# Two non-local attention blocks on one core: other slots for the weight-preparation steps, and the odd pair normalised one slot later

## The chip, the cores and the metric

The kernel runs on one core of a Trainium2 chip. The metric is the device time of one launch in microseconds (us), the median of several runs.

## The reference

Four images of 128 channels by 96 x 96 pixels pass through two layers, one after the other. Each layer is a non-local block:

```
g_x   = maxpool2(conv1x1(x, g_w, g_b))          # 64 channels, 2304 keys
theta = conv1x1(x, theta_w, theta_b)            # 64 channels, 9216 queries
phi   = maxpool2(conv1x1(x, phi_w, phi_b))      # 64 channels, 2304 keys
attn  = softmax(theta^T phi)                    # per query, over the 2304 keys
y     = attn g_x
out   = batchnorm(conv1x1(y, W_w, W_b)) + x     # inference batch norm: a scale and a shift
```

Everything is float32. Batch norm folds into the weights: W is scaled by `inv = gamma * rsqrt(var + eps)`, and all the biases become one shift per channel.

## The kernel before, in words

There are eight blocks, an image with a layer each, in the order of `ORDER`: image 0 layer 0, image 1 layer 0, image 0 layer 1, and so on. A block's 9216 queries are split into nine **pairs** of 1024 queries, 72 pairs in all. For a pair, the 2304 keys are 18 tiles of 128. A **slot** handles two key tiles of one pair, so a pair takes nine slots (NB), and a **cycle** is 18 slots: an even pair in slots 0 to 8 and an odd pair in slots 9 to 17. There are 36 cycles, 648 slots. The main loop runs over the slots `t`, with `s` the slot in its cycle and `q` the first pair of the cycle; what it writes down is the order of each engine's instructions, which no scheduler changes (the schedule is manual).

In each slot TensorE (PE) makes the scores of two key tiles (`sc`, L600), ScalarE (ACT) takes their exponential into one of six `exp` buffers (L605), VectorE (DVE) adds them to the running denominators (`sum`, L612 and L614), and PE multiplies the values of the slot before into `av` (L622). Around this, other work is hung on fixed slots:

- **Units.** While a block runs, the keys and values of the next one are made in six units (`Unit`), two a cycle in the cycles that have any. A unit has four PE stages (L450, L456) in slots 15, 16, 0, 2 (even units) or 7, 8, 10, 12 (odd units), each followed by DVE additions that read its two PSUM banks: L472; L483 twice; L493, L494, L495; L505, L506. Then come two poolings (L510) and DVE transposes (L552). The sums of pixels that the stages read are made by DMAs of SP (L430 to L435) and by accumulating DMAs of GpSimd (POOL, L427).
- **The end of a pair.** ACT copies `av` to `halves` (L629). DVE turns and adds the denominators (`turn`, L672, L673, slots 8 and 9 for the even pair, 4 and 5 for the odd one of the cycle before), adds the two halves of `av` (L705, slots 12 and 2), inverts (L685 to L690, slots 13 and 6), and SP spreads the inverses over the partitions (L694, L698). Then `normalise` multiplies them in (L708, slot `NORM`: 1 for the even pair of the cycle before, 10 for the odd one), PE projects with W (`multiply`, L714, slots 3 and 13), ACT adds the shift (L725) and a POOL DMA adds the result to x (L729).
- **The two PSUM banks** of the tag `misc` serve the unit stages, the theta projections (L277) and the W projections in turn: L714 of slot 3 follows the fourth unit stage of slot 2 in them, and L714 of slot 13 that of slot 12, so it can't start before L505 and L506 have read them.
- **Weights.** The layers' weights are loaded and then turned and scaled in short **steps**, which a dictionary `after` hangs on the end of slots. Layer 0: `mixed` in slots 7, 8, 9 and W in slots 10 to 14 of cycle 0 (`make_scale` L187 to L189, two steps of four 32x32 transposes L150, an ACT copy L228, `make_shift` L235 to L243). Layer 1: 14 steps (`gphi` 4, `mixed` 3, `theta` 2, W 5), three a cycle in slots 2, 7 and 11 of cycles 1 to 5. A step of `gphi`, of `theta` and two of those of W are four DVE transposes; `mixed` is three ACT copies, five small DVE operations and one ACT copy. `load_W` of layer 1 (SP, L171 and L173) stands at slot 16 of cycle 0; it overwrites a buffer that `make_shift` of layer 0 reads.

Within a slot, DVE gets its work in this order: the additions, with those of a unit stage after the first of them; `normalise`, `turn`, `add_halves`, `invert`; the poolings and transposes of units; the steps.

```
for i, step in enumerate(ws[0].steps_W()):
    after[10 + i] = [step]
...
for i, step in enumerate(steps):
    after[CYCLE + i // 3 * CYCLE + (2, 7, 11)[i % 3]] = [step]
```

Of the kernel before, what the change touches and what calls it, by code (L numbers as in the profile page):

```python
# [48 lines left out]


TURNS, HALVES, INVERT = (8, 4), (12, 2), (13, 6)
NORM, PROJECT = (1, 10), (3, 13)
SQ = 32
EXPS = 6
WARM = (5, 3)
CYCLE = 2 * NB
# [6 lines left out]
def shifted_blocks(ctx: ExitStack, tc: tile.TileContext, x: bass.AP, layers, out: bass.AP, flag):  # L63
# [24 lines left out]
    nc = tc.nc  # L88
# [706 lines left out]
    ws = [Layer(l, p) for l, p in enumerate(layers)]  # L795
# [65 lines left out]
    after = {8: [other_cols]}  # L861
    for i, step in enumerate(ws[0].steps_mixed()):
        after[7 + i] = after.get(7 + i, []) + [step]
    for i, step in enumerate(ws[0].steps_W()):
        after[10 + i] = [step]
    after[9] += [lambda: ws[1].load_gphi((nc.sync, nc.sync)), lambda: ws[1].load_theta(nc.sync)]
    after[16] = [lambda: ws[1].load_W(nc.sync)]
    steps = [lambda i=i: late_steps("gphi", i) for i in range(4)]
    steps += [lambda i=i: late_steps("mixed", i) for i in range(3)]
    steps += [lambda i=i: late_steps("theta", i) for i in range(2)]  # L870
# [3 lines left out]
    def late_steps(what, i):  # L874
        if i == 0:
            made[what] = getattr(ws[1], f"steps_{what}")()
        made[what][i]()

    for i, step in enumerate(steps):
        after[CYCLE + i // 3 * CYCLE + (2, 7, 11)[i % 3]] = [step]  # L880

    keys = {2 * j: (0, FIRST + j) for j in range(NB - FIRST)}
    squares = {k: [(1, k)] for k in range(4)} | {5: [(2, k) for k in range(4)]}
# [37 lines left out]
    for t in range(total + 1):  # L921
# [6 lines left out]
        if t in keys:  # L928
            n, i = keys[t]
# [16 lines left out]
        if t < total:  # L946
# [3 lines left out]
            if t in loads:  # L950
                b, i = loads[t]
# [333 lines left out]
def nonlocal_blocks(tc: tile.TileContext, x: bass.AP, layers, out: bass.AP):  # L1285
    with tc.tile_pool(name="flag", bufs=1) as pool:
        flag = pool.tile([1, 1], I32, name="flag")
        shifted_blocks(tc, x, layers, out, flag)
        bad = tc.nc.values_load(flag[0:1, 0:1])
        with tc.If(bad > 0):  # L1290
            general_blocks(tc, x, layers, out)
# [30 lines left out]
```

## Time and profile before

| | |
|---|---|
| time, median of 3 runs | 2484.16 us (2483.57 to 2484.65) |
| the profiled execution's own time | 2483.91 us |
| its span in the profile | 2482.1 us |
| granted TensorE clock in it | 0.999 |
| PE, busy | 2472.2 us, 23391 matmuls |
| PE weight loads, busy | 1602.5 us |
| DVE, busy | 2192.5 us, 2947 instructions |
| ACT, busy | 1667.2 us, 1836 instructions |
| POOL, busy | 254.2 us, 286 instructions |

The profile is of one execution. Matmuls overlap each other and the profile models their ends, so the busy time of PE says that it nearly always had something in it and not that it worked at its full pace; for that, the starts of its matmuls are counted in a stretch. "PEld" is the load of a matmul's weights. "L614 <- ACT exp L605" in a view of waits means that the instruction of line 614 was released by one of ACT of line 605. A time in a view is counted from the start of the span.

### The profile page before, as it was taken

The page shows a single profiled execution, that of the slowest core. Times are in us where ns is not written, and L with a number is a line of the kernel's source. Part 1 is how long each engine was busy: PE and PEld are TensorE (multiplying, and loading weights), DVE is VectorE, ACT ScalarE, POOL GpSimd, SP SyncE. Part 2 cuts the span into 40 slices and gives each one's busy share as a digit, 9 for nine tenths or more (in the row PEclk, how much of TensorE's full clock was granted, in tenths as well). Part 3 has the DMA queues.
Part 4 walks back from the last instruction along what each step waited for, and adds up shares of the span by engine and source line. Part 5 has one row for each costly group of instructions (what it writes and reads, how often), then busy time and mean ns, then how long its engine had stood idle before and what let it go on. Part 6 is the DMA issues. An engine that isn't in the chain of part 4 may idle for free.

```text
span 2482.1 us, 56196 instructions
## 1 busy us (share of the span) xinstructions
PE 2472.2 (100%) x23391; PEld 1602.5 (65%) x23391; DVE 2192.5 (88%) x2947; ACT 1667.2 (67%) x1836; POOL 254.2 (10%) x286
## 2 busy tenths in 40 slices
PE   9999999999999999999999999999999999999998
PEld 5556555666666666666666666666666666666665
DVE  7999989998789988999878998899988899877778
ACT  6666666666667666666666666666666666666665
POOL 0011011100011101111001110111101111000000
PEclk9999999999999999999999999999999999999999
DMA  6366456543356636664346663665424565333334
GB/s 186 45 83 101 52 84 79 81 47 27 36 74 99 101 38 93 89 89 78 44 47 79 84 99 44 94 83 68 49 26 51 77 85 88 42 44 44 44 37 60
DMA packets 101038, 171.72 MB, mean 69 GB/s; under 512 B 16030, under 2 KB 78120, under 8 KB 100776
## 3 DMA queue, kind: packets, MB, share of 16 engines
q1 hardware_dynamic: 65664, 94.11, 31.0%
q0 software_dynamic: 34944, 73.88, 19.6%
q8 instruction: 185, 3.03, 0.5%
q14 instruction: 77, 0.63, 0.1%
q10 hardware_dynamic: 168, 0.07, 0.0%
HBM read 19.21 MB, written 18.87 MB: 15 GB/s over the span
## 4 chain that ended last, share of the span: by engine, by line
PE 94%; DVE 4%; DMA 1%; issue 1%; ACT 0%; SPq 0%; DVEq 0%; POOL 0%; POOLq 0%; ACTq 0%
PE av L622 42%; PE sc L600 42%; PE unit_ps L450 3%; PE theta_ps L277 2%; PE W_ps L714 2%; DVE sum L614 2%; DMA halves<-stage 1%; PE unit_ps L456 0%; PE gphi_ps L329 0%; ACT exp L605 0%; PE gphi_ps L277 0%; DVE four L685 0%; DVE turned L672 0%; DVE stage L510 0%; DVE parts L673 0%
## 5 line engine op out<-in xcount | busy, mean ns | idle before, releaser
L605 ACT ACTIVATE exp<-sc,nshift 128x1024 f32<-128x1024 f32 x1296 | 1391.6, 1112 | 732.8 <-PE sc L600 702.6
L614 DVE TENSOR_TENSOR sum<-sum,exp 128x1024 f32<-128x1024 f32 x1151 | 1408.1, 1223 | 205.5 <-ACT exp L605 149.3
L600 PE MATMUL sc<-theta,phi 64*64 64x512 f32 x10368 | 1459.7, 589 | 0.9 <-ACT exp L605 0.9
L622 PE MATMUL av<-exp,gT 64*64 64x512 f32 x10368 | 1386.2, 589 | 0.0
L622 PEld LDWEIGHTS av<-exp,gT 64*64 64x64 f32 x10368 | 717.5, 133 | 379.4 <-issue 49.8
L600 PEld LDWEIGHTS sc<-theta,phi 64*64 64x64 f32 x10368 | 716.2, 133 | 371.2 <-issue 41.8
L427 POOL DMA_DIRECT2D sums<-x x84 | 81.2, 1140 | 1029.6 <-DMA sums<-x 496.9
L729 POOL DMA_DIRECT2D x<-halves x70 | 62.7, 895 | 1056.3 <-ACT halves L725 1034.5
L612 DVE TENSOR_TENSOR sum<-exp,exp 128x1024 f32<-128x1024 f32 x72 | 88.0, 1222 | 30.0 <-ACT exp L605 29.8
L673 DVE TENSOR_REDUCE parts<-turned 128x16 f32<-128x512 f32 x142 | 97.4, 686 | 4.9
L672 DVE STREAM_TRANSPOSE turned<-sum 128x512 f32<-128x512 f32 x142 | 100.2, 706 | 0.5
L629 ACT COPY halves<-av 128x1024 f32<-128x1024 f32 x71 | 72.0, 1014 | 35.4 <-PE av L622 35.4
L427 POOL DMA_DIRECT2D sums<-sums x84 | 90.9, 1082 | 32.5 <-issue 10.3
L714 PE MATMUL W_ps<-halves,WT 64*64 64x512 f32 x568 | 90.8, 590 | 0.4 <-DVE stage L505 0.4
L277 PE MATMUL theta_ps<-x,thetaT 64*64 64x512 f32 x560 | 89.9, 589 | 0.0
L725 ACT ACTIVATE halves<-W_ps,shift 128x512 f32<-128x512 f32 x140 | 88.6, 692 | 0.9 <-PE W_ps L714 0.9
L450 PE MATMUL unit_ps<-sums,mixed 64*64 64x384 f32 x504 | 78.9, 482 | 0.0
L510 DVE TENSOR_REDUCE stage<-stage 128x192 f32<-128x768 f32 x84 | 77.9, 941 | 0.0
L552 DVE STREAM_TRANSPOSE gT<-stage 32x192 f32<-32x192 f32 (+1 forms) x224 | 71.5, 319 | 3.8
L685 DVE STREAM_TRANSPOSE four<-parts 32x32 f32<-32x32 f32 x284 | 56.4, 198 | 2.9
L708 DVE TENSOR_TENSOR halves<-halves 128x512 f32<-128x512 f32 x71 | 48.8, 687 | 8.9 <-DMA halves<-stage 8.8
L714 PEld LDWEIGHTS W_ps<-halves,WT 64*64 64x64 f32 x568 | 39.7, 133 | 23.0 <-DVE stage L505 2.2
(113 smaller groups left out, 812.7 us busy)
## 6 DMA issues: line engine op xcount, KB each, us to landing
x<-halves POOLq DMA_DIRECT2D x70, 512.0 KB, 4.7
halves<-stage SPq DMA_DIRECT2D x284, 64.0 KB
out_dram<-x SPq DMA_DIRECT2D x35, 512.0 KB
sums<-x SPq DMA_DIRECT2D x42, 384.0 KB
sums<-x SPq DMA_DIRECT2D x84, 192.0 KB
sums<-x POOLq DMA_DIRECT2D x84, 192.0 KB, 4.3
sums<-sums POOLq DMA_DIRECT2D x84, 192.0 KB, 4.6
x<-in_x_dram SPq DMA_DIRECT2D x18, 768.0 KB
```

Source lines behind the costliest of these rows:

```text
L277: nc.tensor.matmul(out, lhsT=lhsT, rhs=rhs, start=step == 0, stop=step == 1)
L427: nc.gpsimd.dma_start(out=dst, in_=src, accum_op=ALU.add)
L450: nc.tensor.matmul(bank[ts(c, CI), :UN], lhsT=lhsT, rhs=rhs[:, c, :], start=True, stop=True)
L600: nc.tensor.matmul(ps[ts(c, CI), ts(h, QT)], lhsT=self.blk.keys_of(k, c, h), rhs=self.th[ts(h, CI), :], start=True, stop=True,)
L605: nc.scalar.activation(e, ps, AF.Exp, bias=nshift)
L612: nc.vector.tensor_add(self.sum, self.es[0], e)
L614: nc.vector.tensor_add(self.sum, self.sum, e)
L622: nc.tensor.matmul(self.av[ts(h, CI), ts(r, QT)], lhsT=self.blk.gT[ts(r, CI), k, :], rhs=e[ts(r, CI), ts(h, QT)], start=(k == 0), stop=(k ...
L672: nc.vector.transpose(self.turned, self.sum[:, ts(h, QT)])
L673: nc.vector.tensor_reduce(self.parts[:, ts(h, QT // SQ)], self.turned.rearrange("p (b k) -> p b k", k=SQ), AX.X, ALU.add,)
L714: nc.tensor.matmul(self.pss[h][ts(c, CI), :], lhsT=self.blk.w.W[ts(h, CI), ts(c, CI)], rhs=self.y[ts(h, CI), :], start=True, stop=True,)
L725: nc.scalar.activation(self.halves[:, ts(h, QT)], self.pss[h], AF.Identity, bias=self.blk.w.shift,)
```

## The change

Three things move; no instruction is added or removed.

- `make_shift` of layer 0 goes from slot 14 to slot 17 of cycle 0, and `load_W` of layer 1 goes with it from slot 16 to slot 17.
- The 14 steps of layer 1 stand two a cycle in slots 1 and 17, in cycles 1 to 7, where they stood three a cycle in slots 2, 7 and 11, in cycles 1 to 5.
- The odd pair of the cycle before is normalised in slot 11 and not in slot 10, in every cycle from 1 on.

```
-NORM, PROJECT = (1, 10), (3, 13)
+NORM, PROJECT = (1, 11), (3, 13)
...
     for i, step in enumerate(ws[0].steps_W()):
-        after[10 + i] = [step]
+        after[(10, 11, 12, 13, 17)[i]] = [step]
     after[9] += [lambda: ws[1].load_gphi((nc.sync, nc.sync)), lambda: ws[1].load_theta(nc.sync)]
-    after[16] = [lambda: ws[1].load_W(nc.sync)]
+    after[17] += [lambda: ws[1].load_W(nc.sync)]
...
     for i, step in enumerate(steps):
-        after[CYCLE + i // 3 * CYCLE + (2, 7, 11)[i % 3]] = [step]
+        after[CYCLE + i // 2 * CYCLE + (1, 17)[i % 2]] = [step]
```

## The prediction

> **What bounds the kernel now.** I read the page first, then the timeline of ACT at the cycles' first exponentials, then the waits of PE, then single slots.
>
> ```profile
> PE 2472.2 (100%) x23391; PEld 1602.5 (65%) x23391; DVE 2192.5 (88%) x2947; ACT 1667.2 (67%) x1836; POOL 254.2 (10%) x286
> ...
> PE 94%; DVE 4%; DMA 1%; issue 1%; ACT 0%; SPq 0%; DVEq 0%; POOL 0%; POOLq 0%; ACTq 0%
> ```
>
> PE is always busy and makes 94% of the chain that ended last. Whether a busy PE is at its pace shows in the cycles' lengths. The chain of work has 16 matmuls of 512 columns in 1.72 us, 0.1075 each, so a slot (32) takes 3.44 and a cycle's 18 slots 61.9; its theta and W projections are 32 more, 3.4: 65.4. The cycle without units from 575.06 to 640.29 took 65.23. The one from 706.49 has six unit stages of 8 matmuls of 384 columns and two of 8 of 192, worth (36 + 6) x 0.1075 = 4.5: 69.9 by count, 69.76 measured. So an ordinary cycle is PE's work at full pace, with no wait to win. Now the early cycles beside ordinary ones of the same work:
>
> ```profile
> 88.69 1.12 ACT L605 ACTIVATE exp<-sc,nshift 128x1024 f32<-128x1024 f32 x1 [1.31 <-PE sc L600]
> 160.41 1.11 ACT L605 ACTIVATE exp<-sc,nshift 128x1024 f32<-128x1024 f32 x1 [1.31 <-PE sc L600]
> 230.70 1.11 ACT L605 ACTIVATE exp<-sc,nshift 128x1024 f32<-128x1024 f32 x1 [1.31 <-PE sc L600]
> 300.32 1.11 ACT L605 ACTIVATE exp<-sc,nshift 128x1024 f32<-128x1024 f32 x1 [1.31 <-PE sc L600]
> 366.52 1.11 ACT L605 ACTIVATE exp<-sc,nshift 128x1024 f32<-128x1024 f32 x1 [1.31 <-PE sc L600]
> 436.52 1.11 ACT L605 ACTIVATE exp<-sc,nshift 128x1024 f32<-128x1024 f32 x1 [1.31 <-PE sc L600]
> ...
> 706.49 1.11 ACT L605 ACTIVATE exp<-sc,nshift 128x1024 f32<-128x1024 f32 x1 [1.31 <-PE sc L600]
> 776.25 1.11 ACT L605 ACTIVATE exp<-sc,nshift 128x1024 f32<-128x1024 f32 x1 [1.31 <-PE sc L600]
> 846.00 1.11 ACT L605 ACTIVATE exp<-sc,nshift 128x1024 f32<-128x1024 f32 x1 [1.31 <-PE sc L600]
> 914.78 1.11 ACT L605 ACTIVATE exp<-sc,nshift 128x1024 f32<-128x1024 f32 x1 [1.31 <-PE sc L600]
> ```
>
> The first lines open cycles 1 to 6, the last four cycles 10 to 13. Differences: cycle 1 took 71.72 against 69.76 for cycle 10, **1.96** too long; cycle 2 70.29 against 69.75 for cycle 11, **0.54**; cycle 3 69.62 against 68.78 for cycle 12, **0.84**; cycle 4 66.20, as cycle 9 (706.49 - 640.29), nothing; cycle 5 70.00 against 69.76, **0.24**. Together 3.58. In cycle 0, slot 16 took 4.39 (exponentials at 80.87 and 85.26), against 3.76 in cycle 9 (699.30 to 703.06): **0.63**. All of it lies where steps stand. What PE waits for in these places:
>
> ```profile
> PEld unit_ps L456 <- DVE stage L472: 3.6, 10, 0.9
> ...
> PEld W_ps L714 <- DVE stage L505: 2.2, 2, 1.1
> ```
>
> Both are PSUM banks that a late DVE frees late. In slot 12 and 13 of cycle 1:
>
> ```profile
> 138.10 0.85 DVE L150 STREAM_TRANSPOSE gphiT<-gphi_nat 32x32 f32<-32x32 f32 x4
> 138.98 1.23 DVE L614 TENSOR_TENSOR sum<-sum,exp 128x1024 f32<-128x1024 f32 x1
> 140.12 0.55 DVE L505 TENSOR_TENSOR stage<-stage,unit_ps 128x384 f32<-128x384 f32 x1
> ```
> ```profile
> 140.72 1.12 PE L714 MATMUL W_ps<-halves,WT 64*64 64x512 f32 x5 [0.23 <-DVE stage L505]
> ```
>
> The step of slot 11 (0.85) stands ahead of L505, and the projection starts 0.05 after L505 ends. In ordinary cycles L505 ends 1.1 to 1.6 before it.
>
> **The Trainium skill against this reading.** Trace Analysis, section Identifying the Most-Contended Engine, calls the busy time of matmuls a poor measure and wants the busy time of weight loads. By it PE (65%) would have a third of each cycle to win, some 24 us of 69.76, an estimate from that page. The count of matmuls above says that there is none; the sum goes by the count.
>
> **The change, part by part.**
>
> *make_shift from slot 14 to 17 of cycle 0.* Its five instructions hold DVE from 79.42 to 80.32, 0.90, just ahead of L472, which ends at 82.01 and is what L456 waits for at 82.06 (weight load 0.95 idle). Without them L472 ends at 81.1. PE's score matmul before that wait starts at 81.40, so L456 comes due 0.1 later and finds its bank free: the 0.63 goes.
>
> *Steps out of slots 2, 7 and 11.* DVE's delay builds up where its work has no gaps. A step in slot 2 still stood as 0.95 before slot 7's L472, a step of slot 7 came on top, and slot 11 lies right before L505. With the steps elsewhere DVE is where it is in cycles 10 to 12, and the 3.58 go.
>
> *Steps into slot 17.* In an ordinary cycle (slots 17, 0 and 1):
>
> ```profile
> 707.11 0.56 DVE L493 TENSOR_TENSOR stage<-stage,unit_ps 128x384 f32<-128x384 f32 x1 [0.34 <-PE unit_ps L450]
> ...
> 709.14 1.23 DVE L612 TENSOR_TENSOR sum<-exp,exp 128x1024 f32<-128x1024 f32 x1 [0.36 <-ACT exp L605]
> 711.77 2.56 DVE L614 TENSOR_TENSOR sum<-sum,exp 128x1024 f32<-128x1024 f32 x2 [1.40 <-ACT exp L605]
> ```
>
> The brackets are DVE idle. A pair's first key tile needs no addition, so there is room: 0.34 + 0.36 + 1.40 = 2.10 for a step of 0.85 to 1.2. L493 to L495 end some 0.5 later, at 709.2, and the stage that needs their banks is in slot 2, after 714. Cost 0, at most 0.5 each without that cover.
>
> *Steps into slot 1*, behind L708:
>
> ```profile
> 714.25 0.68 DVE L708 TENSOR_TENSOR halves<-halves 128x512 f32<-128x512 f32 x1
> 715.15 1.23 DVE L614 TENSOR_TENSOR sum<-sum,exp 128x1024 f32<-128x1024 f32 x1 [0.22 <-ACT exp L605]
> ...
> 719.23 2.56 DVE L614 TENSOR_TENSOR sum<-sum,exp 128x1024 f32<-128x1024 f32 x2 [0.19 <-ACT exp L605]
> ```
>
> Four transposes (0.85) here in cycles 1, 2, 5 and 6 put L505 and L506 back by 0.85 - 0.22 = 0.63. L714 of slot 3 starts at 718.47; L505 would end at 717.48, L506 at 717.94. Still 0.5 early: no wait. After the 0.19, 0.44 is left. In cycles 1 and 5 nothing takes it up before slot 7, since DVE runs without gaps from 721.70 on: L472 there ends at 738.29 and would at 738.73, L456 starts at 739.08 and its weight load, now at 739.08 too, would not wait. Cost 0 to 0.1 each; 0.44 each in two cycles if L456 needs more lead than 0.35. In cycles 3, 4 and 7 the step is ACT copies (0.24 to 0.30 each, three, one and one), under ACT's 1.3 of idle before an exponential.
>
> *Odd normalise from slot 10 to 11*, 0.69 in each cycle. Slot 10 also has L493 to L495; slot 11 then has it in place of a step. Between the two places stand two additions, so L505 in slot 12 has the same work before it. In a cycle like 12 DVE has no real gap from slot 9 to 14 and the swap is neutral; in one like 10 it may idle up to 0.6 in slot 11 that it used before, but L505 has at least 1.1 to spare. What waits for L708 is L714 in slot 13; L708 ended 4.0 to 6.2 before it, and the shift is a slot, 3.4: at least 0.6 is left. Gone are DVE's waits for the DMA that spreads the inverses (8.8 in 13 times), but no PE wait hung on them. Price 0; between a gain of 8.8 and a loss of 0.69 a cycle, I take 0 because ordinary cycles have nothing to win.
>
> *load_W at slot 17.* L173 must now wait for L237, which ends near 89.5, and took 2.32 on SP; behind it stands L430, issued at 89.34. It goes out 0.3 to 2.5 later, and with it POOL's sums (last of them at 104.43), which PE reads in slots 8 and 10, from 121 on. Cost 0. The weights themselves come two cycles later: `gphi` by slot 17 of cycle 2 for slot 15 of cycle 4, `mixed` by slot 1 of cycle 4 for slot 16, W by cycle 7 for cycle 9. All in time.
>
> **Sum.** 2483.91 (the profiled execution's own time) - 3.58 - 0.63 = 2479.7. The median shown lies 0.25 above that execution; I say **2479.8**.
>
> **Rivals.**
> - *Half of it stays.* The 0.44 that slot 1 leaves in DVE reaches L456 in slot 8 or, through the late L510 of slot 14, the unit stage of slot 15. For: that is how cycle 5 lost 0.24 from one step in slot 7. Against: the gaps above. Then some 2 of the 4.2 remain: 2481.8.
> - *More than the floor by count.* The records of matmuls are not complete, and 0.1 of PE idle a cycle in the 35 that move L708 could be hidden: 3.5 more, 2476.3. Against: cycle 8 agrees with its count.
> - *Slower.* L708 in slot 11 delays L505 by its full 0.69 where DVE already lags, and L714 of slot 13 waits in each of the 21 cycles with odd units. It decides from a delay of 1.1 on (cycles like 12) or 1.6 (10 and 11), where L505 ends as L714 starts. Full price 21 x 0.69 = 14.5, less 4.2: 2494. Against: what leaves slot 10 enters slot 11, so the delay is about 0.
> - *The change does nothing there.* The order of the instructions shows the transposes between L708 and L614 of slot 1, so it does what it says.
>
> **Chances.** Forecast 0.64, half 0.20, more 0.12, slower 0.04. Range 2478.6 to 2482.4: the forecast with its bounds (four waits of 0.1 to 0.4, 1 us of spread among runs) and the half case. 0.2% is 4.97 us, about what a measurement of this kernel can tell from no change; the bound, 2479.2, is only 0.6 under the forecast. Faster: the 0.12 and 0.08 of the forecast's 0.64, 0.20; slower 0.04; within 0.76.
>
> **What would show it.** Cycles 1, 2, 3 and 5 at 69.76, 69.75, 68.78 and 69.76; slot 16 of cycle 0 at 3.8; the waits of L714 for L505 gone and those of L456 for L472 down to about 1; cycles from 6 on unchanged. Wrong, if a wait of L714 in slot 3 or of L456 in slot 8 appears in cycles 1, 2, 5 or 6, or if ordinary cycles change at all.

## The result and the profile after

The changed kernel took 2478.68 us against 2483.85 for the kernel before in the same runs: ratio 0.9979 (95% interval 0.9972 to 0.9987). Measured once more it was 2478.78 against 2483.25, ratio 0.9982 (0.9973 to 0.9991). So the medians are 4.5 to 5.2 us apart, where 4.2 was forecast; the first interval, in us, runs from 3.2 to 7.0. The profiled execution took 2478.91, its span is 2477.1.

The page of the changed kernel, the same two lines as before:

```profile
PE 2468.4 (100%) x23391; PEld 1244.7 (50%) x23391; DVE 2193.3 (89%) x2947; ACT 1671.3 (67%) x1836; POOL 254.4 (10%) x286
...
PE 99%; DMA 0%; DVE 0%; ACT 0%; SPq 0%; issue 0%; DVEq 0%
```

The counts are the same, and DVE's share of the chain that ended last fell from 4% to 0%. The timeline of ACT in the changed kernel, at the openings of cycles 1 to 6:

```profile
87.81 1.12 ACT L605 ACTIVATE exp<-sc,nshift 128x1024 f32<-128x1024 f32 x1 [1.31 <-PE sc L600]
157.56 1.12 ACT L605 ACTIVATE exp<-sc,nshift 128x1024 f32<-128x1024 f32 x1 [1.31 <-PE sc L600]
227.31 1.12 ACT L605 ACTIVATE exp<-sc,nshift 128x1024 f32<-128x1024 f32 x1 [1.31 <-PE sc L600]
296.10 1.11 ACT L605 ACTIVATE exp<-sc,nshift 128x1024 f32<-128x1024 f32 x1 [1.31 <-PE sc L600]
362.30 1.12 ACT L605 ACTIVATE exp<-sc,nshift 128x1024 f32<-128x1024 f32 x1 [1.31 <-PE sc L600]
432.06 1.12 ACT L605 ACTIVATE exp<-sc,nshift 128x1024 f32<-128x1024 f32 x1 [1.31 <-PE sc L600]
```

Cycles 1 to 5 now take 69.75, 69.75, 68.79, 66.20 and 69.76, each the length of its ordinary counterpart. Cycle 0 is 0.64 shorter, all of it in slot 16. Cycles 6 to 35 have not changed by 0.01 us. From the first exponential to the one that opens the last slot it is 2440.27 in place of 2444.49: **4.22 less**.

The waits of PE's weight loads in the changed kernel, for the banks that DVE frees (before, L456 waited 3.6 for L472 and L714 2.2 for L505):

```profile
PEld W_ps L714 <- DVE stage L506: 0.4, 2, 0.2
PEld unit_ps L456 <- DVE stage L472: 0.2, 1, 0.2
```

The two of L714 stand in slot 3 of cycles 2 and 5, where the prediction said that a wait would prove it wrong. They are gaps of 0.19, as many weight loads of this profile have for no releaser (for L714 alone 140 such gaps, 30.5 us in all), and both cycles have their ordinary length: they cost nothing.

And slots 12 and 13 of cycle 1, on DVE and on PE:

```profile
135.78 1.22 DVE L614 TENSOR_TENSOR sum<-sum,exp 128x1024 f32<-128x1024 f32 x1
136.92 0.55 DVE L505 TENSOR_TENSOR stage<-stage,unit_ps 128x384 f32<-128x384 f32 x1
```
```profile
139.10 1.13 PE L714 MATMUL W_ps<-halves,WT 64*64 64x512 f32 x8
```

No step stands ahead of L505; it ends at 137.47, and the projection starts 1.6 later without a wait, where it had started 0.05 later.

**The part that was not forecast: the tail.** From the opening of the last slot to the first matmul of the last denominators it is 3.28 in place of 3.69, **0.41 less**. DVE in the last cycle and PE behind it, before:

```profile
2446.17 0.69 DVE L708 TENSOR_TENSOR halves<-halves 128x512 f32<-128x512 f32 x1 [1.56 <-DMA halves<-stage]
...
2449.16 13.16 DVE L614 TENSOR_TENSOR sum<-sum,exp 128x1024 f32<-128x1024 f32 x10
```
```profile
2467.14 0.65 PE L639 MATMUL den_last_ps<-sum,ones 128*64 128x256 f32 x4 [0.34 <-DVE sum L614]
```

and after:

```profile
2444.89 0.68 DVE L708 TENSOR_TENSOR halves<-halves 128x512 f32<-128x512 f32 x1
2445.49 5.21 DVE L614 TENSOR_TENSOR sum<-sum,exp 128x1024 f32<-128x1024 f32 x4
2451.61 2.56 DVE L614 TENSOR_TENSOR sum<-sum,exp 128x1024 f32<-128x1024 f32 x2 [0.90 <-ACT exp L605]
```
```profile
2462.26 0.65 PE L639 MATMUL den_last_ps<-sum,ones 128*64 128x256 f32 x4
```

In slot 10 of the last cycle L708 came before the inverses had landed, and DVE stood for 1.56. It then had ten additions without a gap and was still behind when PE needed the last sum (0.34). One slot later the inverses are there; DVE gets ahead (the 0.90 is idle time) and PE doesn't wait.

### The profile page after: what moved, and what is told of

It reads as the page before. It is cut to its first block, busy times and chain, and to the rows that moved or that the text cites. A ratio compares the mean times of both kernels' runs of the same rounds, so it can differ in the third digit from the quotient of the medians.

```text
span 2477.1 us, 56200 instructions
## 1 busy us (share of the span) xinstructions
PE 2468.4 (100%) x23391; PEld 1244.7 (50%) x23391; DVE 2193.3 (89%) x2947; ACT 1671.3 (67%) x1836; POOL 254.4 (10%) x286
## 4 chain that ended last, share of the span: by engine, by line
PE 99%; DMA 0%; DVE 0%; ACT 0%; SPq 0%; issue 0%; DVEq 0%
PE sc L600 45%; PE av L622 45%; PE unit_ps L450 3%; PE W_ps L714 2%; PE theta_ps L277 2%; PE unit_ps L456 1%; PE gphi_ps L329 0%; PE gphi_ps L277 0%; DMA x<-in_x_dram 0%; PE den_last_ps L639 0%; DVE x L773 0%; PE W_ps L758 0%; ACT exp L605 0%; PE theta_ps L568 0%; PE theta_ps L580 0%; SPq L163 0%
## 5 line engine op out<-in xcount | busy, mean ns | idle before, releaser
L600 PE MATMUL sc<-theta,phi 64*64 64x512 f32 x10368 | 1327.3, 589 | 0.4 <-ACT exp L605 0.4
L622 PE MATMUL av<-exp,gT 64*64 64x512 f32 x10368 | 1273.0, 589 | 0.0
L622 PEld LDWEIGHTS av<-exp,gT 64*64 64x64 f32 x10368 | 550.1, 133 | 547.8 <-issue 527.5
L600 PEld LDWEIGHTS sc<-theta,phi 64*64 64x64 f32 x10368 | 558.8, 133 | 526.5 <-issue 486.4
L612 DVE TENSOR_TENSOR sum<-exp,exp 128x1024 f32<-128x1024 f32 x72 | 88.0, 1222 | 27.4 <-ACT exp L605 27.2
L725 ACT ACTIVATE halves<-W_ps,shift 128x512 f32<-128x512 f32 x140 | 88.7, 693 | 0.0
L277 PE MATMUL theta_ps<-x,thetaT 64*64 64x512 f32 x560 | 77.9, 589 | 0.0
L510 DVE TENSOR_REDUCE stage<-stage 128x192 f32<-128x768 f32 x84 | 77.9, 941 | 0.0
L714 PE MATMUL W_ps<-halves,WT 64*64 64x512 f32 x568 | 77.9, 589 | 0.0
L450 PE MATMUL unit_ps<-sums,mixed 64*64 64x384 f32 x504 | 73.3, 482 | 0.0
L708 DVE TENSOR_TENSOR halves<-halves 128x512 f32<-128x512 f32 x71 | 48.6, 685 | 0.0
L705 DVE TENSOR_TENSOR halves<-halves 128x512 f32<-128x512 f32 x71 | 48.6, 685 | 0.0
```

The lines of the kernel that those rows point to most:

```text
L277: nc.tensor.matmul(out, lhsT=lhsT, rhs=rhs, start=step == 0, stop=step == 1)
L450: nc.tensor.matmul(bank[ts(c, CI), :UN], lhsT=lhsT, rhs=rhs[:, c, :], start=True, stop=True)
L600: nc.tensor.matmul(ps[ts(c, CI), ts(h, QT)], lhsT=self.blk.keys_of(k, c, h), rhs=self.th[ts(h, CI), :], start=True, stop=True,)
L612: nc.vector.tensor_add(self.sum, self.es[0], e)
L622: nc.tensor.matmul(self.av[ts(h, CI), ts(r, QT)], lhsT=self.blk.gT[ts(r, CI), k, :], rhs=e[ts(r, CI), ts(h, QT)], start=(k == 0), stop=(k ...
L714: nc.tensor.matmul(self.pss[h][ts(c, CI), :], lhsT=self.blk.w.W[ts(h, CI), ts(c, CI)], rhs=self.y[ts(h, CI), :], start=True, stop=True,)
```

## The experiments

"Cycles" is the time from the first exponential to the opening of the last slot, "tail" from there to the first matmul of the last denominators, both against the kernel before (2444.49 and 3.69); "time" is the median against that of the kernel before in the same runs. The expectations speak of another stretch, 18.65 and 18.12 from the opening of the last slot to the end of the span. That stretch is 17.94 in e5, which moved nothing in it, so it can't carry a difference of 0.5.

| | cycles | tail | time | ratio, 95% interval |
|---|---|---|---|---|
| changed kernel, first / again | -4.22 / -4.21 | -0.41 / -0.41 | -5.17 / -4.47 | 0.9979 (0.9972 to 0.9987) / 0.9982 (0.9973 to 0.9991) |
| e1 normalise only | +0.64 | -0.41 | +0.39 | 1.0001 (0.9992 to 1.0010) |
| e2 steps only | -4.22 | -0.02 | -4.19 | 0.9983 (0.9974 to 0.9992) |
| e3 normalise, last cycle only | +0.02 | -0.41 | -0.38 | 0.9999 (0.9990 to 1.0008) |
| e4 changed, but not in the last cycle | -4.21 | -0.03 | -4.16 | 0.9983 (0.9974 to 0.9992) |
| e5 make_shift only | -0.97 | -0.03 | -0.86 | 0.9997 (0.9988 to 1.0007) |
| e6 steps in 0, 1, 17 | -4.10 | -0.41 | -4.66 | 0.9981 (0.9972 to 0.9991) |
| e7 steps in 7, 11 | +0.12 | -0.41 | -0.16 | 0.9999 (0.9990 to 1.0009) |
| e8 both steps in 1 | -2.73 | -0.41 | -2.76 | 0.9988 (0.9978 to 0.9998) |
| e9 steps in 2, 17 | -4.15 | -0.41 | -4.44 | 0.9983 (0.9971 to 0.9994) |
| e10 steps in 11, 17 | -3.16 | -0.41 | -3.16 | 0.9986 (0.9975 to 0.9998) |
| e11 before, with slot 11's steps in 17 | -2.15 | -0.02 | -1.44 | 0.9992 (0.9981 to 1.0004) |

Many of these differences are no larger than the intervals. The verdicts rest on the cycles' lengths in the profiles, which are the same to 0.03 us wherever the order of the instructions is the same.

**Which part brings what: e1 to e4.**

```
e1   before, with NORM = (1, 11)
e2   changed, with NORM = (1, 10)
e3   before, with    if s == (11 if i and q == late else NORM[i]):
e4   changed, with   if s == (10 if i and q == late else NORM[i]):
```

e1: 

> The kernel before, with only the odd pair's normalise moved from slot 10 to 11. Theory (the gain is in the stretches with steps, and the missing 0.5 us in the tail): cycles 1, 2, 3 and 5 keep their 71.72, 70.29, 69.62 and 70.00 us, since the same work stands before L505; the last cycle no longer has DVE wait 1.56 for the inverses, and the stretch from the last exponential to the end of the span shrinks from 18.65 to 18.12; about 0.5 faster, 2483.4. Rival (the move is worth something in each cycle): ordinary cycles shorter by 0.1 each, 3.5 faster.

e2: 

> The changed kernel, with the odd pair's normalise back in slot 10; the steps stay in slots 1 and 17. Theory: cycles 0, 1, 2, 3 and 5 as in the changed kernel (69.10, 69.75, 69.75, 68.78, 69.75), so 4.2 faster than before; the tail as before, 18.65; 2479.5. Rival (the move of normalise is needed to clear the way to L505 in slot 12): cycles 1 and 5 keep a part of their 1.96 and 0.24, since slot 1 leaves DVE 0.44 late there; 1 to 2 us slower than that.

e3: 

> The kernel before, with the odd pair normalised in slot 11 in the last cycle alone. Theory: all that the move of normalise brings is here: the same time as with the move in every cycle, 0.5 faster than before, tail 18.12. Rival (the tail shrank for another reason, or by chance of the run): tail 18.65, no change.

e4: 

> The changed kernel, with the odd pair normalised in slot 10 in the last cycle alone. Theory: cycles as in the changed kernel, tail 18.65 as before; 0.5 slower than the changed kernel, 2479.2. Rival: no difference to the changed kernel, 2478.7.

e2 has the whole 4.22 of the cycles and none of the tail, e3 the 0.41 of the tail and none of the cycles, e4 is e2 again: the steps make the cycles shorter, and the move of normalise does its work in the last cycle alone. e1 missed: cycles 1, 2 and 3 grew by 0.2 each (71.93, 70.52, 69.81), which is more than the tail brings. In slot 13 of its cycle 1:

```profile
140.97 1.12 PE L714 MATMUL W_ps<-halves,WT 64*64 64x512 f32 x5 [0.43 <-DVE stage L505]
```

where the kernel before had 0.23. With L708 out of slot 10, DVE reaches the additions of slot 11 early and idles for their exponentials; L708 then stands behind them, next to the step, and L505 ends 0.25 later. Cycles 4 and 6 to 35 did not change. So the move costs where slot 11 has a step and slot 12 the last stage of an odd unit.

**make_shift alone: e5.**

```
-        after[10 + i] = [step]
+        after[(10, 11, 12, 13, 17)[i]] = [step]
...
-    after[16] = [lambda: ws[1].load_W(nc.sync)]
+    after[17] += [lambda: ws[1].load_W(nc.sync)]
```

> The kernel before, with only make_shift of layer 0 and load_W of layer 1 moved to slot 17 of cycle 0. Theory: slot 16 of cycle 0 falls from 4.39 to 3.76, cycle 1 and all later ones stay; 0.63 faster. Rival (what L456 waits for in slot 16 is late for another reason, or load_W holds up SP): slot 16 stays at 4.39, or slot 0 of cycle 1 grows.

Slot 16 of cycle 0 went back to 3.76, as the theory has it, 0.63. Another 0.34 came in slots 8 and 13 of cycle 1 (71.37), which was not expected. At the opening of cycle 1 DVE stands equally far behind the exponentials in both kernels; from slot 3 on it is 0.35 nearer in e5 (2.18 in place of 2.53). One wait of DVE makes the difference. It stands in slot 3 of cycle 1 in the kernel before; e5 has none there, and one like it in slot 3 of cycle 7:

```profile
103.71 1.23 DVE L614 TENSOR_TENSOR sum<-sum,exp 128x1024 f32<-128x1024 f32 x1 [0.46 <-ACT halves L725]
```
```profile
519.76 1.23 DVE L614 TENSOR_TENSOR sum<-sum,exp 128x1024 f32<-128x1024 f32 x1 [0.46 <-ACT halves L725]
```

All kernels with `make_shift` in slot 14 (before, e1, e3, e11) have it in cycle 1; in those with `make_shift` in slot 17 it stands later, in cycle 34 of the changed kernel, or nowhere (e7), and in cycle 34 it costs nothing. With it, L472 of slot 7 of cycle 1 ends 0.94 later than in cycle 10, and slot 8 is 0.26 longer; without it (e5) 0.60 later, and slot 8 has its ordinary length. Why it stands where it does is open.

**The slot, or how many a cycle: e6 to e8.** The changed line in each:

```
e6   after[CYCLE + i // 3 * CYCLE + (0, 1, 17)[i % 3]] = [step]
e7   after[CYCLE + i // 2 * CYCLE + (7, 11)[i % 2]] = [step]
e8   both steps of a cycle appended to slot 1
```

e6: 

> The changed kernel, with layer 1's steps three a cycle again (cycles 1 to 5), in slots 0, 1 and 17. Theory (the slot decides, not how many a cycle): the steps of slot 0 run in DVE's 1.40 of idle time in slot 1; all cycles at the lengths of the changed kernel, 2478.7. Rival (two a cycle is what makes the difference): cycle 1 keeps 1 us or more of its 1.96, total 1 to 2 slower.

e7: 

> The changed kernel, with layer 1's steps two a cycle (cycles 1 to 7) in slots 7 and 11. Theory (the slot decides): the step of slot 11 still lies ahead of L505, and that of slot 7 ahead of the poolings; cycles 1, 2, 3, 5 and 6 lose 0.2 to 1.5 each, 2 to 4 slower than the changed kernel. Rival (two a cycle decides): the cycles of the changed kernel.

e8: 

> The changed kernel, with both steps of a cycle in slot 1: some 1.7 us of DVE there in place of 0.85. Theory (slot 1 has room for one): L505 is put back by about 1.5, L506 ends after its bank is due, so L714 of slot 3 waits 0.1 to 0.4 in cycles 1, 2, 5 and 6, and with 1.3 left in DVE L456 of slot 8 waits 0.3 to 0.6 in cycles 1 and 5; 1 to 3 slower than the changed kernel. Rival (slots 1 to 3 have room enough, and the place does not matter): the cycles of the changed kernel.

Three a cycle in good slots lose 0.11 (cycle 5), two a cycle in the old slots lose 4.34 against the changed kernel: the slot decides, not the count. In e8 slot 1 is too small, as expected: slot 3, where L714 waits, is 0.14, 0.27 and 0.13 longer in cycles 1, 2 and 6, and slot 8, where L456 waits, 0.33, 0.27 and 0.24 in cycles 1, 5 and 6 (a wait in slot 3 of cycle 5 was expected too, and none in slot 8 of cycle 6). Cycle 1 of e8 on PE's weight loads:

```profile
100.45 0.13 PEld L714 LDWEIGHTS W_ps<-halves,WT 64*64 64x64 f32 x1 [0.33 <-DVE stage L505]
121.62 0.14 PEld L456 LDWEIGHTS unit_ps<-stage,mixed 64*64 64x64 f32 x2 [0.65 <-DVE stage L472]
```

**One old slot at a time: e9 to e11.**

```
e9    changed, with (2, 17)[i % 2]
e10   changed, with (11, 17)[i % 2]
e11   before, with (2, 7, 17)[i % 3]
```

e9: 

> The changed kernel, with layer 1's steps two a cycle in slots 2 and 17. Theory (a step costs when what it leaves in DVE reaches a PSUM bank that PE waits for): slot 2 lies behind L505 and L506, so L714 of slot 3 is untouched, and what is left, up to 0.95, reaches L472 of slot 7: cycles 1 and 5 lose 0.2 to 0.3 each, the others nothing; 0.5 slower than the changed kernel. Rival (any old slot costs as much as any other): as in slots 7 and 11, 4 us.

e10: 

> The changed kernel, with layer 1's steps two a cycle in slots 11 and 17. Theory: a step of slot 11 lies right before L505 and the poolings of slots 13 and 14, and alone costs 0.6 to 1.2 in each of cycles 1, 2, 5 and 6, where four transposes stand there, and nothing in 3, 4 and 7 (copies on ACT): 3 to 4 slower than the changed kernel, most of what slots 7 and 11 cost together. Rival (it needs the step of slot 7 as well to be late): under 1 slower.

e11: 

> The kernel before, with layer 1's steps of slot 11 moved to slot 17; those of slots 2 and 7 stay, three a cycle. Theory: cycle 1 keeps the 0.26 of its slot 8 and loses its waits in slots 13 to 16, cycles 2 and 3 lose their 0.54 and 0.84; cycle 5, whose steps stand in slots 2 and 7, keeps its 0.24. About 2.8 faster than before. Rival (the steps of slots 2 and 7 carry the delay to slot 13 by themselves): under 1 faster.

e9 lost 0.07, less than expected: slot 2 alone is nearly as good as slot 1. The 0.95 of the expectation was measured in the kernel before, where 0.35 of it comes of the wait for L725 just shown; in e9 L472 of cycle 1 ends 0.60 later than in cycle 10.

e10 missed by far: a step in slot 11 alone costs 0.24, 0.17, 0.35 and 0.30 in cycles 1, 2, 5 and 6, 1.06 in all, and nothing in slot 13. In these cycles L505 still ends 0.74 to 1.05 before L714, so the banks are free in time. With the step of slot 7 as well (e7) it ends 0.06 to 0.52 before it, and slot 13 loses 1.14 over all cycles. L714 needs the second bank too, and L506 ends 0.46 after L505: in e7 slot 13 loses nothing where L505 ends 0.52 before L714, 0.07 at 0.48, 0.17 at 0.39, 0.19 at 0.36 and 0.30 at 0.25. The larger part lies elsewhere: all of e10's 1.06 and 3.2 of e7's 4.34 are lost in slots 14 to 16. (Both kernels have the odd normalise in slot 11 as well, which cost 0.2 a cycle beside a step in e1; no run takes that apart.)

e11 got 2.15 of the 2.8: cycles 2 and 3 are ordinary again, but cycle 1 kept 0.27 in slot 8 and 0.87 in slots 14 to 16. So there is a second way by which a late DVE reaches PE. ACT and PE's weight loads in slots 14 to 16 of cycle 1, kernel before:

```profile
147.99 0.38 ACT L541 ACTIVATE phi<-stage,centre 128x96 f32<-128x96 f32 x1 [0.97 <-DVE stage L510]
...
151.37 0.48 ACT L469 COPY stage<-unit_ps 128x384 f32<-128x384 f32 x1 [0.31 <-DVE stage L510]
```
```profile
151.11 0.36 PEld L600 LDWEIGHTS sc<-theta,phi 64*64 64x64 f32 x8 [0.50 <-ACT exp L605]
151.90 0.43 PEld L456 LDWEIGHTS unit_ps<-sums,mixed 64*64 64x64 f32 x4 [0.43 <-ACT stage L469]
152.92 0.21 PEld L600 LDWEIGHTS sc<-theta,phi 64*64 64x64 f32 x8 [0.59 <-ACT exp L605]
```

and ACT in the same slots of the changed kernel:

```profile
144.93 0.38 ACT L541 ACTIVATE phi<-stage,centre 128x96 f32<-128x96 f32 x1
...
148.31 0.48 ACT L469 COPY stage<-unit_ps 128x384 f32<-128x384 f32 x1 [0.31 <-DVE stage L510]
```

L541 reads what the pooling L510 has made. Before, the pooling is late on DVE, ACT stands for 0.97 in front of L541, and all that is behind it in ACT's queue is late with it: the exponentials, which free the score banks, and L469, for which L456 waits. The 0.31 in front of L469 is there in both kernels and is not the difference. Where unit stages follow in slots 15 and 16, the loss goes with the wait of L541: 0.97, 0.70 and 0.42 in cycles 1, 2 and 5 before, with 0.87, 0.54 and 0.24 lost; 0.35, 0.28, 0.46 and 0.41 in cycles 1, 2, 5 and 6 of e10, with 0.24, 0.17, 0.35 and 0.30 lost. In cycle 3, which has no such stages, L541 waits 0.98, and these slots lose nothing. No run moved the copies of ACT, so this way is read from the traces and not tested by itself.

**The rest of the difference: e12**, the changed kernel again. 

> The changed kernel once more, on a chip with its own runs of the kernel before. Theory: the cycles (4.22) and the tail (0.41) are the whole gain, 4.6 us, and the 5.2 of the first measurement has half a microsecond of the runs' spread in it. Rival: there is a further source of 0.5, and the difference is 5.2 again.

4.47: nothing is left to explain beyond the cycles and the tail (4.63), and the first measurement's other half microsecond lies within the spread of the runs. In the profiles the time to the first exponential alone varies from 18.60 to 19.58 us over kernels with the same code up to there, and the time from the first matmul of the last denominators to the end from 14.28 to 14.99.

## Why the prediction was right, point by point

- **Ordinary cycles are PE's work at full pace.** Right: not one of cycles 6 to 35 changed. The Trainium skill (Perfetto Trace Analysis, section Identifying the Most-Contended Engine) names, beside MFU, the summed slices of the weight loads over the window as the measure of TensorE's headroom. The prediction took the profile's busy time for it (65%), which counts overlapping loads once. The sum itself is 126% of the span in all 14 profiles (23391 loads of 134 ns in the mean), so here it gives no headroom and doesn't tell the kernels apart. The busy share doesn't follow the time either: it fell to 50% in the changed kernel, and is 62% in e6 (2478.8 us) and 51% in e7 (2483.3 us). What fits the cycles is the count of their matmuls.
- **The 3.58 in cycles 1, 2, 3 and 5.** Right, in each cycle: 1.96, 0.54, 0.84, 0.24. The way was half right. Waits for banks that DVE frees are there, in slots 8 and 13 of cycle 1 and slot 13 of cycle 3, and make 1.94 of it. The other 1.65, all of it in slots 14 to 16, came by ACT's queue: 0.87 of cycle 1 and the whole of cycles 2 and 5. The prediction has the late pooling only in a rival, for cycle 5. And 0.34 of cycle 1 did not hang on the steps of layer 1 but went with `make_shift` (e5): the 0.95 that it put down to the step of slot 2 was 0.60 and the wait for L725. The sum did not need any of this, because it compared whole cycles and all the parts moved at once.
- **0.63 for make_shift.** Right in slot 16 (e5); its other 0.34 is inside the 3.58.
- **Steps into slots 17 and 1 at 0 to 0.1.** Right. It was near: L472 of cycle 5 ends at 394.51, and the weight load that waits for it starts at 394.56. Slot 8 is no longer for that; with two steps in slot 1 (e8) it is.
- **Odd normalise at 0.** The step that failed is "no PE wait hung on them". It holds in 34 cycles, but in the last one, where the even pair's inverses are made in the same slot 10, the 1.56 of waiting for the DMA kept DVE behind up to the last sum: 0.41 (e3, e4). And "the swap is neutral" is so only without a step in slot 11: with one it costs 0.2 in cycles 1, 2 and 3 (e1).
- **load_W.** Right: L430 went out 0.6 later in its slot (1.25 after its opening in place of 0.65), and no PE wait came of it.
- **The rivals.** None of them decided. The waits that "half of it stays" fears, in slots 3 and 8, come with twice the work in slot 1: e8 loses 1.49 of the 4.22, 1.4 of it there (2480.7). "More than the floor" is ruled out by cycles 6 to 35, which did not change, and so is "slower".
- **The number.** The prediction's own terms give 2483.91 - 3.58 - 0.63 + 0.25 = 2479.95, not 2479.8. The result is 1.27 under that, close to the lower end of the range: 0.41 is the tail, 0.31 that the kernel before took 2483.85 in these runs and not 2484.16, and 0.55 within the spread of the runs (the second measurement has 4.47 in place of 5.17). That the last two fell on the same side as the tail is chance. The prediction gave 0.76 to a difference within 0.2%; the two measurements have 0.21% and 0.18%.

## What to carry to other kernels

Price a wait by comparing whole periods: a stretch with the suspect work beside a later one with the same work and without it gave 4.2 of 4.6 us at once. The chain priced nothing: its 4% for DVE were some 99 us, and in e8, which loses 1.4 us in slots where PE waits for DVE, it gives DVE 0%. Extra work on an engine beside the bottleneck was free here as long as its delay stayed under the lead of every hand-over behind it, that is, under the time by which the engine was done before the other needed the result. One step in slot 11 was harmless at L714 and cost 1.06 us through ACT's queue (e10); two together cost at both places (e7). So look at all the hand-overs behind such a piece, and put it where that engine idles next, not where it fits the code. Read the last period by itself, since a wait that later work absorbs everywhere else counts there.

## What the runs showed of the hardware that was not expected

- The busy time of weight loads for the same 23391 loads was 1222 to 1612 us over these runs, and did not follow the time: 1531 us in e6 (2478.8 us), 1261 us in e7 (2483.3 us).
- The cycles' lengths repeat to 0.03 us over kernels and chips, while the time to the first exponential varies by 1.0 us.
